# The fifth recurrent step of a four-layer graph network with tokens on the partitions: stationary data, moving weights, and no turn back of the state

## The chip, the core and the metric

The kernel runs on one NeuronCore of a Trainium2 chip. Five engines work side by side from queues of their own: TensorE (PE: matrix products and transposes into PSUM), VectorE (DVE), ScalarE (ACT), GpSimd (POOL) and SyncE (SP, which here only issues DMAs). The metric is the device time of one execution in microseconds. All data are float32.

## The reference, cut to what matters

There are 128 graphs of 64 nodes with 256 features each. Two attention layers come first, then a gated recurrent network (layer 2), then a gated graph convolution (layer 3). Every layer is a residual on a normalised input.

```python
h = relu(layernorm(x));  x = x + attention0(h, adj)
h = relu(layernorm(x));  x = x + attention1(h, adj)
# layer 2, five recurrent steps
h = relu(layernorm(x)); A = (adj != 0)
for l in range(5):
    m   = h @ weight[l]                    # 256 -> 256
    agg = einsum('bij,bid->bjd', A, m)     # sum over the neighbours
    gi  = agg @ w_ih.T + b_ih;  gh = h @ w_hh.T + b_hh     # 256 -> 3*256: r, z, n
    r, z = sigmoid(gi_r + gh_r), sigmoid(gi_z + gh_z)
    n   = tanh(gi_n + r * gh_n)
    h   = (1 - z) * n + z * h
x = x + h * nodemask
# layer 3
h = relu(layernorm(x)); norm = (sum(|adj|, -1) + 1e-6) ** -0.5
f_hom = adj @ ((h @ theta) * norm) * norm
gate  = sigmoid(h @ W_t + b_t)
x = x + elu(gate * f_hom + (1 - gate) * (h @ W_h))
```

## The kernel before, in words

Two graphs make a pair of 128 tokens, four pairs make a group of 512 tokens (`TOK`; `HALF` is 256), and there are 16 groups. `front(g)` does the two attention layers of group g, `entry` the normalisation ahead of the recurrent layer, `gru` its five steps (a generator that yields after each), and `back` layer 3 and the store.

The order of the instructions is written by a planner in the kernel (`class Plan`). Every operation is added with its engine, a cost in ns, what it reads and writes, and a due time (`key`). `strand` spreads the due times of a block over a share of a group's length. `Plan.run` then emits the operations in the order in which its own costs say that they can start, ties going to the earlier due time. The recurrent step l of group g has its due time at g + 0.4 l, so two groups are always inside the recurrent layer, and attention of a later group and layer 3 of an earlier one fill TensorE in between. The constants `FRONT_SPAN`, `BACK`, `STEP` and `LOCK` set these due times. The last group (`LOCK`) is drawn nearer to the one before.

Tiles come from `new(tag, shape, n)`: n buffers under a tag; a value waits until a buffer of its tag is free. There are four PSUM banks with tag `g` for the recurrent products (called `nb`, `gb`, `gc`, `nc` here) and four with tag `a` for everything else.

Inside the recurrent layer the state `h` lies with features on the partitions: `h[128 features, 2, 512 tokens]`. The products keep a 128x128 block of weights stationary and move 256 tokens of data (line 994). They use Strassen's scheme on 2x2 blocks: seven block products instead of eight, numbered 1 to 7, with the sums of data blocks in `Th` (of `h`) and `Ta` (of the aggregate), and sums of weight blocks prepared once in `w_hh` and `gv`. A block product is six matmuls in a step: r, z and n, each from `h` and from the aggregate. After a product an intermediate bank is copied to SBUF by ACT (`saved`, line 1058) and later added to another bank by DVE (`summed`, lines 1066 and 1069).

`update` (lines 1086 to 1107) then forms the gates and the new state for one half of the features: tanh on ACT with the bias b_rz, two DVE operations, tanh on ACT, a subtraction on POOL (line 1103), two DVE operations. After each step but the fifth, `turned` transposes `h` into `ht`, tokens on the partitions, because the aggregation `agg` (line 1034) wants it so. The last group's fifth step goes by halves of the tokens (`by_halves`, `update_half`) so that layer 3 can start on one half earlier.

Layer 3 wants tokens on the partitions. So `back_half` transposes the final `h` with TensorE into a PSUM tile `hx` (line 1375), and DVE adds it times the mask to x (line 1382). Layer 3 also needs each pair's adjacency as a block-diagonal 128x128 matrix, transposed: at the end of `front`, POOL copies the two 64x64 blocks into `blk` (line 1265), TensorE transposes them (line 1280) and ACT scales them into `adjT` (line 1285). `adjT` has four buffers, since it waits there until `back`, more than a group's length later.

The first groups also load and prepare the weights. SP issues nearly all DMAs from one queue, in the planner's order: among them the prepared gate weights `gv` once per step (line 977) and the attention weights `qw` (line 626).

Of the kernel before, what the change touches and what calls it, by code (L numbers as in the profile page):

```python
# [23 lines left out]
P = 128  # L24
# [37 lines left out]
FRONT_SPAN = 0.95  # L62
BACK = -0.1
BACK_LAST = 0.3
BACK_SPAN = 0.7
STEP = 0.0
STEP_LAST = -0.1
STEP_SPAN = 0.5
LOCK = 0.35
# [24 lines left out]
def act(n, ptr=0):  # L94
    return n * 0.833 + 60 + 105 * ptr
# [193 lines left out]
def network(ctx: ExitStack, tc: tile.TileContext, a: dict, out: bass.AP, flag):  # L289
# [99 lines left out]
    with plan.strand(-3.0, 0.1):  # L389
# [46 lines left out]
        first = [new("h", [P, 2, 2, D], 4, f"w_{n}") for n in ("qk0", "qk1", "v")]  # L436
# [21 lines left out]
        for c, tag in enumerate(("ht", "agg")):  # L458
            t = new(tag, [P, 3 * D], 2 if tag == "ht" else 1, f"w_ih{c}")
            dma(384, lambda c=c, t=t: nc.sync.dma_start(  # L460
                t.tile, a["L2_gnn_w_ih"][c * P : (c + 1) * P, :]), [], [t])
            w_ih.append(t)
# [42 lines left out]
    with plan.strand(-0.3, 0.1):  # L505
# [19 lines left out]
        b_t = load_row("L3_gnn_b_t")  # L525
        blk = filled("adjblk", [P, PAIRS, P], 0.0)
# [384 lines left out]
    def fuse_weights(l):  # L911
# [14 lines left out]
        for mc in range(2):  # L926
            for g0, n in ((0, 2), (2, 1)):
# [7 lines left out]
                def put(copy, mc=mc, g0=g0, n=n, ps=ps):  # L935
                    copy(gv[:, g0 : g0 + n, 2 * mc : 2 * mc + 2, :],
# [14 lines left out]
    def gru(h, ht, A, name, last=False):  # L951
# [20 lines left out]
        for l in range(LAYERS):  # L972
# [45 lines left out]
            hn(1, hi_b, True)  # L1018
            rz_h(1, rz_b, True)
            rz_h(2, rz_c, True)  # L1020
            hn(2, hi_c, True)
            Ta = new("Ta", [P, 4, HALF], 1, f"Ta_{nm}")

# [51 lines left out]
            ht2 = None if l + 1 == LAYERS else new("ht", [P, PAIRS, D], 2, f"ht_{nm}")  # L1075
# [34 lines left out]
            def turned(oc, ht2=ht2):  # L1110
                if ht2 is not None:
                    transposed(ht2, lambda: ht2[:, :, oc * P : (oc + 1) * P], h, lambda i: h[:, oc, i * P : (i + 1) * P],
                        f"hT_{nm}_{oc}", oc == 0, [(ht2, oc)],
                        reads=[(h, (oc, 0)), (h, (oc, 1))], width=P)

            def update_half(half, g_v, n_v, last=None):

                r, z, a_, b_ = (lambda v=v, k=k: v[:, :, k, :] for v in (g_v, n_v) for k in range(2))
                hh = lambda: h[:, :, half * HALF : (half + 1) * HALF]
                hp = [(h, (oc, half)) for oc in range(2)]  # L1120
                for k in range(2):
                    for oc in range(2):
                        src, at = (g_v, lambda k=k, oc=oc: g_v[:, oc, k, :]) if last is None or not oc else (
                            last, lambda k=k: last[:, k * HALF : (k + 1) * HALF])
                        col = 2 * k + oc
                        sca(act(HALF, 1.4), lambda k=k, col=col, oc=oc, at=at: nc.scalar.activation(
                            g_v[:, oc, k, :], at(), AF.Tanh, bias=b_rz[:, col : col + 1], scale=0.5),
                            [(src, oc) if src is g_v else src, b_rz], [(g_v, f"t{k}{oc}")])
                ts = [[(g_v, f"t{k}{oc}") for oc in range(2)] for k in range(2)]
                vec2(dve(TOK), lambda: nc.vector.scalar_tensor_tensor(  # L1130
                    a_(), r(), 1.0, a_(), op0=ALU.add, op1=ALU.mult), [*ts[0], n_v], [n_v])
                vec2(dve(TOK), lambda: nc.vector.scalar_tensor_tensor(
                    a_(), a_(), 0.5, b_(), op0=ALU.mult, op1=ALU.add), [n_v], [n_v])
                for oc in range(2):
                    sca(act(HALF, 1.4), lambda oc=oc: nc.scalar.activation(
                        n_v[:, oc, 0, :], n_v[:, oc, 0, :], AF.Tanh, bias=b_n[:, oc : oc + 1]), [n_v, b_n], [(n_v, oc)])
# [397 lines left out]
```

## Time and profile before

| | before |
|---|---|
| median of 6 runs | 2502.55 us (2501.34 to 2503.53) |
| the profiled execution | 2501.24 us |
| its span, first to last instruction | 2499.4 us |
| granted TensorE clock | 0.998 |
| PE / DVE / ACT / POOL busy | 2477.0 / 1881.6 / 1308.4 / 896.0 us |
| DMA, mean over the span | 75 GB/s |

A group line of the profile reads: source line, engine, operation, output<-inputs, shapes, count, then busy us and the mean ns of one, then the engine's idle time just ahead of them and who ended it. The count of a float32 matmul is two per matmul; a transpose counts once. The busy time of TensorE overlaps from one matmul to the next, so its pace is read from the starts in the timeline, not from the mean length of one. A timeline line reads: start, length, engine, source line, operation, output<-inputs, shapes, count.

### The profile page before, as it was taken

The numbers are of one execution on the slowest core, as the hardware profiler recorded it, in microseconds if no ns is written. First come the engines' busy times: TensorE is split into PE (matmuls) and PEld (weight loads), VectorE is DVE, ScalarE is ACT, GpSimd is POOL, SyncE is SP. The second block draws the span as 40 slices with busy tenths as digits, with TensorE's granted clock in tenths as the row PEclk, the third lists the DMA queues.
The fourth block names the chain that finished last, engine by engine and source line by source line (L and its number), as shares of the span: only waits on it lengthen the run. The fifth ranks groups of instructions, "written<-read, shape, count | busy, mean of one in ns | idle before, by whom it ended". The sixth has DMA issues, their size and how long they took to land.

```text
span 2499.4 us, 58765 instructions
## 1 busy us (share of the span) xinstructions
PE 2477.0 (99%) x24057; PEld 2130.3 (85%) x24057; DVE 1881.6 (75%) x4396; ACT 1308.4 (52%) x2654; POOL 896.0 (36%) x894
## 2 busy tenths in 40 slices
PE   9999999999999999999999999999999999999997
PEld 7788888888888888888888888888888888888885
DVE  6667777777777777787778777787777777777776
ACT  3455554555555455555555555555454555645544
POOL 5633433334233342433334233343333424332221
PEclk9999999999999999999999999999999999999999
DMA  6422212112222121212113122122211212212110
GB/s 210 159 71 86 72 53 99 65 53 84 72 80 72 60 76 66 98 54 80 59 63 102 50 95 76 52 82 72 80 68 60 76 66 80 68 50 71 51 69 19
DMA packets 78266, 188.60 MB, mean 75 GB/s; under 512 B 14802, under 2 KB 66852, under 8 KB 67108
## 3 DMA queue, kind: packets, MB, share of 16 engines
q1 hardware_dynamic: 77872, 184.71, 22.0%
q8 instruction: 192, 3.15, 0.5%
q14 instruction: 86, 0.70, 0.1%
q10 hardware_dynamic: 116, 0.04, 0.0%
HBM read 166.70 MB, written 18.02 MB: 74 GB/s over the span
## 4 chain that ended last, share of the span: by engine, by line
PE 98%; DVE 1%; ACT 1%; issue 0%; DMA 0%; POOL 0%; DVEq 0%; ACTq 0%
PE gb L994 22%; PE gc L994 17%; PE nb L994 11%; PE nc L994 8%; PE qkvb L711 6%; PE qkvc L711 5%; PE y L879 4%; PE agg L1034 3%; PE l3b L1339 3%; PE s L775 3%; PE l3c L1339 2%; PE hT L547 2%; PE lnT L547 2%; PE o L843 2%; PE o L851 1%; PE gv L930 1%
## 5 line engine op out<-in xcount | busy, mean ns | idle before, releaser
L1103 POOL TENSOR_TENSOR sn<-h,sn 128x512 f32<-128x512 f32 x158 | 202.9, 1287 | 544.5 <-ACT sn L1101 544.5
L533 POOL TENSOR_TENSOR rstd<-pw,few 128x2 f32<-128x2 f32 x128 | 96.3, 755 | 490.0 <-DVE pw L532 445.2
L994 PE MATMUL gb<-Th,w_hh 128*128 128x256 f32 x960 | 249.3, 382 | 0.0
L994 PE MATMUL gb<-Ta,gv 128*128 128x256 f32 x960 | 246.8, 380 | 0.0
L963 POOL TENSOR_TENSOR Th<-h 128x256 f32<-128x256 f32 x160 | 121.2, 777 | 299.6 <-PE nb L994 196.2
L799 POOL TENSOR_TENSOR e<-e,mask 128x512 f32<-128x512 f32 x128 | 177.4, 1406 | 111.5 <-ACT e L797 111.4
L994 PEld LDWEIGHTS gb<-Ta,gv 128*128 128x128 f32 x960 | 177.6, 190 | 22.1 <-issue 0.2
L994 PEld LDWEIGHTS gb<-Th,w_hh 128*128 128x128 f32 x960 | 175.7, 190 | 23.9 <-issue 2.4
L1101 ACT ACTIVATE sn<-sn,b_n 128x512 f32<-128x512 f32 x158 | 114.0, 722 | 143.8 <-DVE sn L1099 143.8
L1105 DVE SCALAR_TENSOR_TENSOR sn<-sg,sn 128x512 f32<-128x512 f32 x158 | 120.5, 769 | 74.4 <-POOL sn L1103 74.2
L994 PE MATMUL gc<-h,w_hh 128*128 128x256 f32 x640 | 167.7, 384 | 0.1
L994 PE MATMUL gc<-agg,gv 128*128 128x256 f32 x640 | 164.3, 379 | 0.0
L1086 ACT ACTIVATE sg<-sg,b_rz 128x512 f32<-128x512 f32 x158 | 106.5, 714 | 81.2 <-DVE sg L1066 81.2
L963 POOL TENSOR_TENSOR Th<-h,Th 128x256 f32<-128x256 f32 x160 | 144.9, 906 | 8.4 <-DVE h L1107 2.8
L552 ACT ACTIVATE hT<-lnT 128x512 f32<-128x512 f32 x96 | 57.1, 594 | 167.1 <-PE lnT L547 167.0
L994 PE MATMUL nb<-Ta,gv 128*128 128x256 f32 x480 | 144.0, 382 | 0.0
L994 PE MATMUL nb<-Th,w_hh 128*128 128x256 f32 x480 | 143.0, 380 | 0.0
L1097 DVE SCALAR_TENSOR_TENSOR sn<-sg,sn 128x512 f32<-128x512 f32 x158 | 117.7, 752 | 32.8 <-ACT sn L1208 28.3
L994 PEld LDWEIGHTS gc<-h,w_hh 128*128 128x128 f32 x640 | 116.2, 190 | 26.6 <-ACT sn L1208 4.0
L1099 DVE SCALAR_TENSOR_TENSOR sn<-sn 128x512 f32<-128x512 f32 x158 | 136.6, 871 | 2.4
L1047 DVE TENSOR_TENSOR Ta<-agg 128x256 f32<-128x256 f32 x160 | 100.2, 643 | 50.6 <-PE nb L994 27.7
L994 PEld LDWEIGHTS gc<-agg,gv 128*128 128x128 f32 x640 | 121.3, 190 | 16.7 <-issue 0.2
(228 smaller groups left out, 6560.4 us busy)
## 6 DMA issues: line engine op xcount, KB each, us to landing
gv<-gates SPq DMA_DIRECT2D x80, 1344.0 KB, 5.9
qw<-kept SPq DMA_DIRECT2D x203, 192.0 KB, 2.4
x<-in_x_dram SPq DMA_DIRECT2D x32, 256.0 KB, 3.0
out_dram<-x SPq DMA_DIRECT2D x32, 256.0 KB, 2.6
gates<-gv SPq DMA_DIRECT2D x5, 1344.0 KB, 5.6
adjq<-in_adj_dram SPq DMA_DIRECT2D x8, 256.0 KB, 4.7
gw<-in_L_gnn_weight_dram SPq DMA_DIRECT2D x5, 256.0 KB, 6.1
kept<-s SPq DMA_DIRECT2D x8, 128.0 KB, 1.8
```

The costliest lines, as they stand in the source:

```text
L711: nc.tensor.matmul(bk[:, j * P : (j + 1) * P], lhs, rhs, start=first and j == 0, stop=True, skip_group_check=True)
L799: pool(1225, lambda e=e: nc.gpsimd.tensor_tensor(e.tile, e.tile, bias_at(pp)[:, None, :].to_broadcast([P, 4, 2 * NODES]), op=ALU.mult), [e ...
L963: pool(690, lambda: nc.gpsimd.tensor_tensor(T[:, i, :], x(), y(), op=ALU.subtract), reads, [(T, i)])
L994: nc.tensor.matmul(bank_[:, col * HALF : (col + 1) * HALF], at(g, n), rhs(), start=first and j == 0, stop=True, skip_group_check=True)
L1047: vec2(dve(256), lambda: nc.vector.tensor_tensor(Ta[:, i, :], x(), y(), op=ALU.subtract), reads, [(Ta, i)])
L1086: sca(act(TOK, 1.5), lambda k=k, col=col: nc.scalar.activation(g_v[:, :, k, :], g_v[:, :, k, :], AF.Tanh, bias=b_rz[:, col : col + 1], sca ...
L1097: vec2(dve(TOK), lambda: nc.vector.scalar_tensor_tensor(a_(), r(), 1.0, a_(), op0=ALU.add, op1=ALU.mult), [*ts[0], n_v], [n_v])
L1099: vec2(dve(TOK), lambda: nc.vector.scalar_tensor_tensor(a_(), a_(), 0.5, b_(), op0=ALU.mult, op1=ALU.add), [n_v], [n_v])
L1101: sca(act(TOK, 1.5), lambda: nc.scalar.activation(a_(), a_(), AF.Tanh, bias=b_n[:, oc : oc + 1]), [n_v, b_n], [n_v])
L1103: pool(1230, lambda: nc.gpsimd.tensor_tensor(b_(), hh(), a_(), op=ALU.subtract), [*hp, n_v], [n_v])
L1105: vec2(dve(TOK), lambda: nc.vector.scalar_tensor_tensor(b_(), z(), 1.0, b_(), op0=ALU.add, op1=ALU.mult), [*ts[1], n_v], [n_v])
L1339: pe(mm(384), lambda: nc.tensor.matmul(bk[:, : 3 * P], b(), w3[:, :, n, :], start=first, stop=True, skip_group_check=True), [w3, *reads], ...
```

## The change

In the fifth step the operands change places. A block of 128 tokens of `h`, `agg`, `Th` or `Ta` is stationary, and the three gates' weights (3x128 columns) move, in `last_step`. A block product is then four matmuls of 384 columns (two blocks of 128 tokens, from `h` and from the aggregate) instead of six of 256. The result has tokens on the partitions, so the final state is formed in `ht`, in place, and `back_half` reads it without a transpose.

- In this layout a bias differs along the columns, so it cannot be ACT's per-partition bias. `load_b` spreads the biases over all partitions once, with six DMAs and one POOL addition into `b_row`. `saved` gets a POOL addition of `b_row` after each copy, six in a step. `summed` is four DVE additions of 256 columns in place of two of 512.
- One tanh of 1024 columns serves r and z of a half. The last group still goes by halves of tokens.
- `gv` of the fifth step holds the gates in the order n, r, z, so that the aggregate's part goes to columns 0 to 383 of a bank, and the state's (r, z, n) to 128 to 511.
- The transposed adjacency is made at the start of `back`. `blk` is filled there by two DMAs from HBM in place of POOL's two copies.
- Buffers: `h` 4 to 3, `ht` 2 to 3, `adjT` 4 to 2. Due times: `FRONT_SPAN` 0.95 to 1.0, `BACK` -0.1 to -0.05, `STEP` 0 to -0.05, `LOCK` 0.35 to 0.3.

```diff
-FRONT_SPAN = 0.95
-BACK = -0.1
+FRONT_SPAN = 1.0
+BACK = -0.05
...
-STEP = 0.0
+STEP = -0.05
...
-LOCK = 0.35
+LOCK = 0.3
...
+        b_row = new("b_row", [P, 2, 4, P], 1)
+        more = new("e", [P, 2, 2, P], 4 if lean else 3, "b_more")
+
+        def load_b():
+            ih, hh = a["L2_gnn_b_ih"], a["L2_gnn_b_hh"]
+            for dst, ap, at, gates in ((b_row[:, :, 0], ih, 2 * D, 0), (b_row[:, :, 3], hh, 2 * D, 0),
...
+                nc.sync.dma_start(dst, bass.AP(tensor=ap.tensor, offset=ap.offset + at, ap=[[0, P], [P, 2], [1, P]]))
+
+        dma(768, load_b, [], [b_row, more], 6)
+        pool(1225, lambda: nc.gpsimd.tensor_tensor(
+            b_row[:, :, 1:3, :], b_row[:, :, 1:3, :], more.tile, op=ALU.add), [b_row, more], [b_row])
...
+            by_token = l + 1 == LAYERS
+            if by_token:
+                tokens = last_step(nm, h, Th, Ta, agg, gv, ((rz_b, hi_b), (rz_c, hi_c)), operand, by_both, whole, last)
+                next(tokens)
+            else:
+                hn(1, hi_b, True)
...
+    def last_step(nm, h, Th, Ta, agg, gv, banks, operand, by_both, whole, halves):
+
+        def product(i, which, of_h, first=False):
+            n = WEIGHTS[i]
+            b, reads = operand(i, h, Th, by_both) if of_h else operand(i, agg, Ta, whole)
+            w = w_hh if of_h else gv
+            for t in range(2):
+                bk = banks[which][t]
+                pe(mm(384), lambda t=t, bk=bk: nc.tensor.matmul(
+                    bk[:, P:] if of_h else bk[:, : 3 * P], b()[:, t * P : (t + 1) * P], w[:, :, n, :],
+                    start=first, stop=True, skip_group_check=True), [w, reads], [bk])
...
+        def saved(which, n, oc):
...
+                sca(act(512), lambda c=c, bk=bk: nc.scalar.activation(
+                    c.tile, bk.tile.rearrange("p (g f) -> p g f", g=4), AF.Copy), [bk], [c])
+                pool(1225, lambda c=c: nc.gpsimd.tensor_tensor(c.tile, c.tile, b_row[:, oc], op=ALU.add),
+                     [c, b_row], [c])
...
+        def summed(oc, half, which, others):
...
+                for dst, key, part in ((sg, "g", lambda x: x[:, 1:3, :]), (sn, "n", lambda x: x[:, 0:4:3, :])):
+                    vec(dve(256), lambda dst=dst, part=part, bk=bk, p=p, o_at=o_at: nc.vector.tensor_tensor(
+                        dst[:, p], part(bk.tile.rearrange("p (g f) -> p g f", g=4)), part(o_at()), op=ALU.add),
+                        [bk, o], [(dst, p)])
...
+        def update(j):
...
+            sca(act(2 * TOK, 0.4), lambda: nc.scalar.activation(sg.tile, sg.tile, AF.Tanh, scale=0.5), parts, [sg])
...
+        if halves:
...
+            both(4, 0)
+            summed(1, 0, 0, None)
+            update(0)
+            both(5, 1, True)
+            summed(1, 1, 1, v)
+            both(3, 1)
+            summed(0, 1, 1, u)
+            update(1)
...
+        both(5, 1, True)
+        p5 = saved(1, "p5", 1)
+        both(6, 0)
+        u = saved(0, "u", 0)
+        both(3, 1)
+        summed(0, 1, 1, u)
+        update(0)
+        both(7, 0)
+        summed(1, 1, 0, p5)
+        both(4, 0)
+        summed(1, 0, 0, None)
+        update(1)
...
-        for gp in range(2):
-            s = slice(gp * NODES, (gp + 1) * NODES)
-            pool(350, lambda s=s: nc.gpsimd.tensor_copy(blk[s, :, s], adjq[s, sel, :]), [adjq], [(blk, gp)])
-
...
+    def back(g, xt, norm):
+
+        def fill():
+            for gp in range(2):
+                s = slice(gp * NODES, (gp + 1) * NODES)
+                nc.sync.dma_start(blk[s, :, s], adj_t[s, g * PAIRS : (g + 1) * PAIRS, :])
+
+        dma(128, fill, [], [blk], 2)
+        adjT = new("adjT", [P, PAIRS, P], 2, f"adjT_{g}")
...
-    def back_half(g, xt, h, adjT, norm, half):
-        ps = bank(f"hx_{g}_{half}")
-
-        def turn():
-            for i in range(2):
-                for c in range(2):
-                    t0 = (2 * half + i) * P
-                    nc.tensor.transpose(ps[:, i * D + c * P : i * D + (c + 1) * P],
-                                        h[:, c, t0 : t0 + P], ident.tile)
-
-        pe(437, turn, [(h, (0, half)), (h, (1, half)), ident], [ps], mode=TURN)
...
-                xt[:, p, :], ps[:, i * D : (i + 1) * D], cols[:, 18 + t : 19 + t], xt[:, p, :],
-                op0=ALU.mult, op1=ALU.add), [ps, cols, (xt, p)], [(xt, p)])
+    def back_half(g, xt, adjT, norm, half):
+        h_by_token = final[g]
+        for p in range(2 * half, 2 * half + 2):
...
+                xt[:, p, :], h_by_token[:, p, :], cols[:, 18 + t : 19 + t], xt[:, p, :],
+                op0=ALU.mult, op1=ALU.add),
```

## The prediction

> **What bounds the kernel now.** I read the page's busy shares and its chain first, then the windows by group, then the starts in TensorE's timeline, then the waits and the groups that the change touches.
>
> ```profile
> PE 2477.0 (99%) x24057; PEld 2130.3 (85%) x24057; DVE 1881.6 (75%) x4396; ACT 1308.4 (52%) x2654; POOL 896.0 (36%) x894
> PE 98%; DVE 1%; ACT 1%; issue 0%; DMA 0%; POOL 0%; DVEq 0%; ACTq 0%
> ```
>
> TensorE is busy nearly always and is 98% of the chain that ended last. The windows (length, then busy us by engine) show that this holds in each stage but the end:
>
> ```profile
> 912.00:1064.00 152.00, 152.00 (x1504) 131.65 (x1503) 117.44 (x278) 81.51 (x168) 54.57 (x54) 1.00 0.22 74
> 1064.00:1216.00 152.00, 152.00 (x1505) 131.83 (x1504) 117.46 (x278) 81.63 (x168) 54.65 (x54) 1.00 0.22 72
> 2432.00:2499.40 67.40, 49.57 (x264) 35.21 (x262) 47.30 (x117) 29.89 (x64) 9.99 (x13) 0.94 0.05 18
> ```
>
> A group takes 152 us and repeats itself; DVE has 34 us of slack in it, ACT 70, POOL 97. The clock is 1.00. What TensorE issues is what a group costs. Its pace stands in the starts:
>
> ```profile
> 329.55 0.81 PE L1339 MATMUL l3c<-w,hTT 128*128 128x384 f32 x2
> 330.20 0.81 PE L1339 MATMUL l3b<-w,hTT 128*128 128x384 f32 x2
> 330.84 0.59 PE L994 MATMUL nb<-Th,w_hh 128*128 128x256 f32 x2
> 331.27 0.81 PE L1339 MATMUL l3c<-w,hT 128*128 128x384 f32 x2
> ...
> 999.71 0.81 PE L994 MATMUL gb<-h,w_hh 128*128 128x256 f32 x3
> 1000.45 1.16 PE L1034 MATMUL agg<-A,ht 64*64 64x64 f32 x64
> ```
>
> Two records of 384 columns take 0.645 us from start to start, so 322.5 ns each; two of 256 take 0.43, so 216 each. The 384 rows are layer 3's: data stationary, weights moving with a stride, which is the form that the fifth step gets. Their weight load (190 ns) hides. The three records ahead of `agg` take 0.74 and not 0.65: entering small tiles costs 0.09 us.
>
> ```profile
> L1375 PE MATMUL hx<-ident,h 128*128 128x128 f32 x128 | 19.2, 274 | 1.4 <-DVE h L1141 1.4
> L1103 POOL TENSOR_TENSOR sn<-h,sn 128x512 f32<-128x512 f32 x158 | 202.9, 1287 | 544.5 <-ACT sn L1101 544.5
> L1047 DVE TENSOR_TENSOR Ta<-agg 128x256 f32<-128x256 f32 x160 | 100.2, 643 | 50.6 <-PE nb L994 27.7 <-ACT sg L1093 20.6 <-ACT agg L1040 2.2
> L1265 POOL COPY adjblk<-adjq 64x256 f32<-64x256 f32 x32 | 19.3, 603 | 4.8 <-PE adjT L1280 3.4 <-DMA adjq<-in_adj_dram 0.4
> PE f L1310 <- ACT hT L552: 2.2, 2, 1.1
> PE hx L1375 <- DVE h L1141: 1.4, 1, 1.4
> ```
>
> The last two are waits (total, times, longest). The usual steps between starts, summed over the order before, make 2439.5 us; first to last start takes 2485.3. So 45.8 us are waits: 9.7 in the first 152 us, 2.7 in the second, 1.4 to 2.0 in each later one, 7.5 after 2432. The end is short of work on TensorE, so chains over DVE and ACT count there. The span of 2499.4 stands in an execution of 2501.24, 1.3 under the median 2502.55; the sum below is made on the span and taken off the median.
>
> **The change, part by part.** First TensorE, counted in the order of both programs.
>
> Fifth step: out go 16 x 42 = 672 matmuls of 256, two records each: 1344 x 216 ns = 290.3 us. In come 16 x 28 = 448 of 384: 896 x 322.5 = 289.0. Net -1.3: the columns are the same, only the fixed few ns become fewer.
>
> The turn back: 128 transposes go. Four of them pace 0.43 us in the timeline, 109 ns each: -13.9. TensorE is the bound where they stand, so all of it counts.
>
> Adjacency: the same 64 transposes, moved from `front` to `back`: 0. Their POOL copies go (32 x 0.60 = 19 us on an engine with slack).
>
> Small tiles: the planner's order of the changed kernel goes 152 times from full to small tiles, before 138. 0.09 on entering, and 0.1 to 0.2 on leaving (148 to 199 ns where one small record follows another in 7 to 38): 14 x 0.2 = +2.8, at most 14 x 0.3 = 4.2.
>
> Sum on TensorE: -1.3 - 13.9 + 2.8 = -12.4 us, or -0.7 us a group.
>
> Other engines, a group. POOL gets 6 additions like L1103 (1.29, mask product 1.41) and loses two copies: 7.7 - 1.2 = +6.5 on 54.7 of 152. DVE gets 16 additions of 256 from PSUM (0.42 each, as layer 3's copy shows) for 6 of 512 (0.69): +2.6 on 117.5. ACT loses a copy of 0.69 and trades eight tanh for four longer ones: -2. None gets near 152: no price by itself, the cover is TensorE's 150 us. What is left is latency.
>
> (1) `saved` is longer by two POOL additions in a row, 2.6 us. After product 1 the order has 11 us of TensorE work before product 5 overwrites the banks: cover enough (copies 1.2 + additions 2.6 + sums 1.4 = 5.2). After product 6 `u` has 4.3 us until the second bank of product 3 is to be summed, against 0.8 + 2.6 plus POOL's queue, where a mask product (1.41) may stand ahead: slack from +0.9 to -0.5. Behind it are the banks that the next group's step starts with, at once. Bounds: 0, and one POOL addition plus what a DVE operation with two SBUF inputs loses (643 - 414 alone = 0.23) less 0.5, so 1.0 a group, 14 us in all. I take 0.15 x 14 = +2, near the low end, since most waits of that length are covered today.
>
> (2) Beside POOL a DVE operation with two SBUF inputs is slow already: L1047 takes 643 ns on average, 414 where no POOL operation overlaps. Twelve percent more POOL work makes the existing excess 12% larger: well under 1 us of DVE's slack.
>
> The Trainium skill (SBUF — State Buffer, section "SBUF: two separate sides") says that VectorE and GpSimd hold their shared port as an exclusive lock for the whole instruction, which speaks against six more POOL additions; if each blocked DVE for its full 1.29 us, an estimate from that rule, DVE would come to 128 of 152 us, still no bound, and the sum would stay -12.4 plus whatever of it lies on a chain.
>
> (3) SP: the fill is two more DMAs a group (64 KB each, 256-byte runs) right behind the turn of the group before, some 140 us of TensorE work ahead of its use. The adjacency load of 256 KB in the same runs lands in 4.7 us. `blk` has one buffer, so SP waits there for that turn, with the next group's `gv` queued behind; 14 us of TensorE steps remain until that group's first product, against 0.9 of issue and `gv`'s 5.9 to land. Price 0; if the turn came 7 us late, `gv` would be late by what is over. The six bias loads stand where SP's timeline is empty (46 to 53 us) and the addition on POOL waits for them: 0, at most their landing of about 4 us. Fewer `h` buffers: the first loads leave theirs by 63 us and `h` is first written near 93.
>
> The Trainium skill (DMA: Bandwidth & Descriptors, section "Specifications") puts line rate at 512 bytes and more; by it the fill is slow, which its 140 us of cover make worth nothing.
>
> (4) The start: `adjT` leaves a stretch with 0.6 of waits, other work is reshuffled: 0, bounds -3 and +3.
>
> (5) The end. From product 4 of the last group to layer 3's turn `lnT` of its first half the trace takes 14.2 us (2457.0 to 2471.2), 12.5 of them TensorE work, 1.7 waits. In the new order only 9.9 us of TensorE work stand there; more was put ahead. The chain loses `hx` and its wait for TensorE (about 1), tanh becomes one of about 0.93 for four of 0.41 to 0.46 (-0.8), and DVE, packed there, gets 12 starts of 256 at 0.34 for 4 of 512 at 0.62 (+1.6). I get 13.3 by walking it, so a wait of 3.4: +1.7 against before. Bounds: 9.9 (no wait, -1.7) and 15.8 (nothing saved, +4.2). The two waits of `f` (2.2) stay.
>
> Sum: -12.4 + 2 + 0 + 1.7 = -8.7, or rounded with the many bounds at zero -9: **2493.5 us**.
>
> **The rivals.** All of TensorE's gain arrives and the chain at the end is no longer than today's: -12.4, perhaps -1.7 on top: 2488.5 to 2490. For it: a group repeats with 1.75 us of waits, most of about 0.1. Against: the thin end.
>
> Slower: `u` waits for POOL in each group. Place: the last sums of product 3 in the fifth step. Price: a whole addition late behind a mask product, 1.41 + 0.23, and the next group's first products with it; 16 x 1.64 = 26 on -12.4 gives 2516. It decides from 0.78 us a group (12.4 / 16). For it: POOL is in order, and DVE waits up to 2.5 us for its L1103 today. Against: POOL is 40% busy and the step has filler.
>
> No change within 0.2% (5 us either way, about what can be told): the same waits at 0.5 to 0.8 a group, or a start and an end both at their upper bounds (+3, +4.2, +1.4 small tiles): 2499 to 2503.
>
> That the turn back was hidden anyway would give 2507 (13.9 less gained); against it, TensorE waits only 1.8% of the time (45.8 of 2485.3), so there is hardly a gap that a transpose could have filled.
>
> **How the numbers follow.** Forecast 0.55 (own range 2490.5 to 2497), full gain 0.22 (2487 to 2490.5), no change 0.13 (2497.5 to 2507), slower 0.10 (2507 to 2520). Two in ten left out are the slow case and half of no change, so 2487 to 2501. Faster than 2497.5: 0.55 + 0.22 + 0.01 = 0.78; same 0.12; slower 0.10.
>
> **What would show it.** Groups that repeat every 151.3 to 151.5 us; no `hx` line; the fifth step's records at 322 ns start to start; TensorE's waits still near 1.8 us a group; a wait of `lnT` or its neighbour of 2 to 5 us at the end. I am wrong if sums of the fifth step stand idle for POOL, with TensorE's `nb` or `gb` of the next step waiting for them, or if the first 300 us grow.

## The result, and the profile after

The changed kernel takes 2508.53 us in the median of 17 runs (2507.28 to 2511.52), the kernel before 2501.76 in 37 (2501.02 to 2503.72). The ratio is 1.0026, with a 95% interval of 1.0020 to 1.0033: it is slower by nearly 7 us (0.26%), where 9 fewer were forecast. The profiled execution took 2507.86 us with a span of 2505.9, at a clock of 0.997.

The first and the fourth part of the page of the changed kernel, the busy shares and the chain that ended last:

```profile
PE 2474.8 (99%) x23481; PEld 2033.3 (81%) x23481; DVE 1920.9 (77%) x4556; ACT 1284.0 (51%) x2570; POOL 990.9 (40%) x959
PE 94%; DVE 2%; issue 1%; ACT 0%; POOL 0%; DVEq 0%; ACTq 0%
```

TensorE has 576 records fewer, and yet its share of the chain fell from 98% to 94%: it waits more. GpSimd (POOL) has 95 us more to do. The windows of the same groups as before (length, then busy time of PE, PEld, DVE, ACT and POOL with their counts, clock, DMA share, GB/s):

```profile
912.00:1064.00 152.00, 151.12 (x1460) 124.81 (x1460) 119.36 (x285) 80.15 (x162) 59.83 (x57) 1.00 0.21 73
1064.00:1216.00 152.00, 151.30 (x1466) 125.32 (x1465) 119.65 (x287) 80.24 (x162) 59.74 (x58) 1.00 0.22 74
2432.00:2505.90 73.90, 56.88 (x256) 35.31 (x254) 55.64 (x135) 31.35 (x64) 20.32 (x20) 0.89 0.05 16
```

Before, TensorE was busy for all of the 152 us of such a window; now 0.7 to 0.9 us are gaps. The waits of TensorE in the changed kernel (engine, what waited, for what: us in total, times, longest) name them:

```profile
PE nb L1012 <- DVE sn L1221: 7.7, 11, 0.7
PE hom L1471 <- DVE F L1391: 2.9, 1, 2.9
PE f L1384 <- ACT hT L567: 1.8, 2, 1.1
```

The first line is new. L1012 is the product of a recurrent step (L994 before), L1221 is `summed` in the fifth step: `nb` of the next group's third step waits for its bank until a sum of the fifth step has read it out, 11 times, once in each of groups 2 to 12. Counted as in the prediction, the usual steps between TensorE's starts sum to 2427.0 us instead of 2439.5, which is 12.5 less; 12.4 was forecast. From the first to the last start 2493.0 us pass instead of 2485.3. So the waits are 66.0 us and not 45.8: +20.2. Of these some 12.9 lie at that place (11 times 1.17, with the products right behind it), 3 to 4 in the last 80 us, up to 1.6 in the first 300 (this goes by what one calls a usual step), and about 3 in late small tiles, of which more below (these overlap by about 1). What follows the last start became 1.2 shorter. -12.5 + 20.2 - 1.2 is the 6.5 by which the span grew.

The place itself, in the timeline of the changed kernel (start, length, engine, line; the groups look alike, this is the change of step near 902 us):

```profile
899.09 2.49 POOL L1209 TENSOR_TENSOR u<-u,b_row 128x512 f32<-128x512 f32 x2
...
901.53 0.71 POOL L548 TENSOR_TENSOR rstd<-pw,few 128x2 f32<-128x2 f32 x1
901.78 0.42 DVE L1221 TENSOR_TENSOR sg<-gc,u 128x256 f32<-128x256 f32 x1 [0.75 <-PE gc L1194]
...
902.12 1.55 DVE L710 TENSOR_TENSOR hTQ<-hT 128x128 f32<-128x128 f32 x2
...
902.21 1.31 POOL L803 TENSOR_TENSOR x<-x,r_L_gnn_bo 128x512 f32<-128x512 f32 x1
...
903.60 0.28 DVE L710 TENSOR_TENSOR hTQ<-hT,hTQ 128x128 f32<-128x128 f32 x1
903.80 0.41 DVE L1221 TENSOR_TENSOR sn<-gc,u 128x256 f32<-128x256 f32 x1
...
904.36 0.67 PE L1012 MATMUL nb<-h,w_hh 128*128 128x256 f32 x2 [0.70 <-DVE sn L1221]
```

Read it from below. `nb` waits for the second sum, `sn<-gc,u`. That sum does not wait for anything: between the two sums VectorE (DVE) has instructions of an attention layer of a later group, the subtractions `hTQ` (L710), whose time is 0.28 each elsewhere. Here two of them take 1.55 (one alone 1.36), and they end at 903.67, just behind GpSimd's addition L803 (903.52). The trace has 11 such subtractions, one at each of the 11 places; all end 0.15 us behind an L803. L803 adds the bias `bo` to x ahead of attention's output (L788 before, called x + bo below). It comes here because GpSimd, which takes its instructions one after the other, is behind: from 899.09 on it has done the two new bias additions of `u` (L1209), an `rstd` (L548) and then L803. And `u` was not late: its additions were over at 901.58, and the first sum waited until 901.78 for TensorE's `gc`.

How far a GpSimd instruction holds one of VectorE shows in two more rows of the trace, the instructions of single tiles with min/median/max in ns. `pw_deg` adds a constant to a tile of 128x4. Before:

```profile
L532 DVE TENSOR_SCALAR pw_deg<-deg x16: 156/158/960, 10.4 to 2020.2; 128x4 f32<-128x4 f32 x16
```

After, in the first row, and below it `hTQ`:

```profile
L547 DVE TENSOR_SCALAR pw_deg<-deg x16: 161/1236/1245, 8.8 to 2055.5; 128x4 f32<-128x4 f32 x16
...
L710 DVE TENSOR_TENSOR hTQ<-hT x116: 248/281/1365, 84.5 to 2221.5; 128x128 f32<-128x128 f32 x116
```

The 11 long `pw_deg` all start 0.3 to 0.6 us behind an L803 and end 0.02 to 0.03 us behind its end. The one that starts 0.02 us ahead of a GpSimd instruction (300.37, the subtraction L1248) takes 169 ns.

### The profile page after: what moved, and what is told of

The parts are those of the page before. It is cut to its first block, busy times and chain, and to the rows that moved or that the text cites. A ratio compares the mean times of both kernels' runs of the same rounds, so it can differ in the third digit from the quotient of the medians.

```text
span 2505.9 us, 57822 instructions
## 1 busy us (share of the span) xinstructions
PE 2474.8 (99%) x23481; PEld 2033.3 (81%) x23481; DVE 1920.9 (77%) x4556; ACT 1284.0 (51%) x2570; POOL 990.9 (40%) x959
## 4 chain that ended last, share of the span: by engine, by line
PE 94%; DVE 2%; issue 1%; ACT 0%; POOL 0%; DVEq 0%
PE gb L1012 18%; PE gc L1012 13%; PE nb L1012 9%; PE nc L1012 7%; PE qkvb L726 6%; PE qkvc L726 4%; PE y L894 4%; PE gb L1194 3%; PE agg L1057 3%; PE nb L1194 3%; PE l3b L1413 3%; PE s L790 3%; PE gc L1194 2%; PE hT L562 2%; PE l3c L1413 2%; PE nc L1194 2%
## 5 line engine op out<-in xcount | busy, mean ns | idle before, releaser
L1126 POOL TENSOR_TENSOR sn<-h,sn 128x512 f32<-128x512 f32 x128 | 163.4, 1277 | 714.7 <-ACT sn L1124 714.2
L548 POOL TENSOR_TENSOR rstd<-pw,few 128x2 f32<-128x2 f32 x128 | 107.6, 841 | 324.1 <-DVE pw L547 314.0
L1012 PE MATMUL gb<-Th,w_hh 128*128 128x256 f32 x768 | 199.9, 383 | 0.0
L1012 PE MATMUL gb<-Ta,gv 128*128 128x256 f32 x768 | 197.6, 380 | 0.0
L1012 PEld LDWEIGHTS gb<-Ta,gv 128*128 128x128 f32 x768 | 143.0, 190 | 23.8
L1012 PEld LDWEIGHTS gb<-Th,w_hh 128*128 128x128 f32 x768 | 140.4, 190 | 21.9 <-issue 4.7
L1128 DVE SCALAR_TENSOR_TENSOR sn<-sg,sn 128x512 f32<-128x512 f32 x128 | 110.1, 860 | 48.9 <-POOL sn L1126 48.7
L894 PE MATMUL y<-w_L_gnn_Wo,oT 128*128 128x256 f32 x512 | 138.4, 380 | 0.1
L1012 PE MATMUL gc<-h,w_hh 128*128 128x256 f32 x512 | 131.9, 380 | 0.2 <-DVE h L1130 0.2
L1012 PE MATMUL gc<-agg,gv 128*128 128x256 f32 x512 | 131.5, 379 | 0.0
L1012 PE MATMUL nb<-Ta,gv 128*128 128x256 f32 x384 | 115.5, 382 | 0.0
L1012 PE MATMUL nb<-Th,w_hh 128*128 128x256 f32 x384 | 114.5, 380 | 0.0
L1070 DVE TENSOR_TENSOR Ta<-agg 128x256 f32<-128x256 f32 x160 | 93.8, 603 | 25.0 <-ACT sg L1116 19.5
L592 DVE TENSOR_SCALAR xn<-x,mv,rstd 128x256 f32<-128x256 f32 x192 | 103.5, 567 | 11.9 <-POOL rstd L548 6.1
L894 PEld LDWEIGHTS y<-w_L_gnn_Wo,oT 128*128 128x128 f32 x512 | 93.0, 190 | 23.3 <-issue 1.2
L726 PEld LDWEIGHTS qkvb<-hTQ,qw 128*128 128x128 f32 x696 | 100.2, 191 | 12.9 <-DVE v L747 0.2
L726 PE MATMUL qkvb<-hTQ,qw 128*128 128x128 f32 x696 | 106.5, 275 | 0.0
```

What stands on the lines that cost most here:

```text
L548: pool(660 if n == 2 else 970, lambda: nc.gpsimd.tensor_tensor(dst.tile, s.tile, few[:, 1 : 1 + n], op=ALU.pow), [s, (few, 1)], [dst], port=2)
L592: vec2(325, lambda p=p, i=i: nc.vector.tensor_scalar(xn[:, i, :], xt[:, p, :], mv_at()[:, i, 0:1], rstd[:, i : i + 1], op0=ALU.subtract, o ...
L726: nc.tensor.matmul(bk[:, j * P : (j + 1) * P], lhs, rhs, start=first and j == 0, stop=True, skip_group_check=True)
L894: pe(mm(256), lambda i=i, c=c: nc.tensor.matmul(py[:, i * D : (i + 1) * D], oT[:, i, c, :], w_o[:, c, :], start=c == 0, stop=c == 1), [(oT ...
L1012: nc.tensor.matmul(bank_[:, col * HALF : (col + 1) * HALF], at(g, n), rhs(), start=first and j == 0, stop=True, skip_group_check=True)
L1070: vec2(dve(256), lambda: nc.vector.tensor_tensor(Ta[:, i, :], x(), y(), op=ALU.subtract), reads, [(Ta, i)])
```

## The experiments

In the texts below, theory A is this: GpSimd comes late to the change of step; its x + bo holds an `hTQ` between two sums that free a bank; `nb` waits. Rivals: the sums wait for the additions themselves (B); TensorE became slower in itself (C); VectorE is too full in any order (D). In the table, "waits" is the time from TensorE's first to last start less its usual steps, in us.

| kernel | median us | ratio to before, 95% | waits |
|---|---|---|---|
| before | 2501.76 | | 45.8 |
| changed | 2508.53 | 1.0026 (1.0020 to 1.0033) | 66.0 |
| x + bo short | 2495.78 | 0.9977 (0.9967 to 0.9987) | 54.2 |
| before, x + bo short | 2503.07 | 1.0003 (0.9994 to 1.0012) | 47.2 |
| bias additions short | 2496.60 | 0.9979 (0.9970 to 0.9988) | 55.8 |
| second sum moved up | 2507.09 | 1.0021 (1.0012 to 1.0030) | 63.4 |
| four sums first | 2499.79 | 0.9992 (0.9983 to 1.0001) | 57.4 |
| pairs of sums planned as one | 2510.45 | 1.0045 (1.0031 to 1.0058) | 69.2 |
| truer costs for the planner | 2521.46 | 1.0077 (1.0063 to 1.0091) | 80.6 |
| old constants | 2520.71 | 1.0076 (1.0063 to 1.0090) | 76.5 |
| x + bo later | 2505.15 | 1.0014 (1.0005 to 1.0023) | 62.7 |
| x + bo later, four sums first | 2513.79 | 1.0046 (1.0032 to 1.0060) | 72.8 |
| no fill of the adjacency | 2508.32 | 1.0026 (1.0016 to 1.0037) | 65.1 |
| four sums first, subtraction on VectorE | 2496.63 | 0.9979 (0.9970 to 0.9988) | 56.2 |
| subtraction on VectorE alone | 2507.27 | 1.0020 (1.0011 to 1.0030) | 64.7 |
| x + bo later, subtraction on VectorE | 2497.50 | 0.9980 (0.9971 to 0.9989) | 53.8 |
| four sums first, subtraction on VectorE, long stretches split | 2496.68 | 0.9979 (0.9970 to 0.9988) | 54.0 |

Where a line of the table says "short", the order of all instructions is that of its parent: the planner was given the same costs. Each ratio is to runs of the kernel before made beside that kernel, with medians between 2501.36 and 2502.16 us; a difference of under 1 us between two lines tells nothing.

**x + bo short.**

```diff
-            xt[:, pp : pp + 2, :], xt[:, pp : pp + 2, :], bo[:, None, :].to_broadcast([P, 2, D]),
+            xt[:, pp : pp + 2, :8], xt[:, pp : pp + 2, :8], bo[:, None, :8].to_broadcast([P, 2, 8]),
```

> The changed kernel with its order of instructions untouched, in which GpSimd's addition x + bo (L803) covers 8 of each row's 256 columns, so that it takes a fraction of its 1.35 us; the other columns go without that bias, and nothing else is changed. Theory A (the port): in the changed kernel this addition runs late, between the two sums of the fifth step that free bank gc, and holds VectorE's second hTQ subtraction for 1.36 us instead of 0.28; TensorE's nb of the next group waits for it, 11 times 1.17 = 12.9 us. Then this run is 11 to 14 us under the changed kernel, about 2496, and the waits of nb on sn are below 0.3 us a group. Rival B (the six additions of b_row are what is late, and the sums wait for them): x + bo stands behind them in GpSimd's queue, and the time stays within 2 us of 2508.5. Rival C (TensorE itself got slower, in its weight loads or its rate): no change either.

2495.78 us, 12.7 less than the changed kernel. The same place in this run's timeline:

```profile
898.11 0.42 DVE L1221 TENSOR_TENSOR sg<-gc,u 128x256 f32<-128x256 f32 x1 [0.75 <-PE gc L1194]
...
898.46 0.50 DVE L710 TENSOR_TENSOR hTQ<-hT 128x128 f32<-128x128 f32 x2
...
898.54 0.27 POOL L803 TENSOR_TENSOR x<-x,r_L_gnn_bo 128x16 f32<-128x16 f32 x1
...
898.88 0.28 DVE L710 TENSOR_TENSOR hTQ<-hT,hTQ 128x128 f32<-128x128 f32 x1
899.08 0.41 DVE L1221 TENSOR_TENSOR sn<-gc,u 128x256 f32<-128x256 f32 x1
```

The pair of `hTQ` takes 0.50 instead of 1.55, the second sum starts 0.97 after the first and not 2.02, and `nb` no longer stands among the waits. Since the order is the same, the starts of TensorE's records in the two traces can be set side by side: this run gains 1.02 to 1.03 us at each of the 11 places, 11.3 us in all (of the 1.17 there, 0.15 stays). It gains 1.0 once more near 147 us, in an ordinary step, where x + bo holds two other VectorE instructions (`Ta`, L1070: 1.92 us together instead of 0.87). C falls, and so does B, since the additions are as long as before.

**The same in the kernel before.** The same edit, at line 788 there.

> The kernel before with the same addition (there L788) on 8 of 256 columns, the other columns going without that bias; its order is untouched. It tells what a short x + bo is worth where it does not stand between two sums. Theory A: within 2 us of 2501.8. If GpSimd's use of the port costs TensorE something everywhere, it gains as much here as in the changed kernel, and theory A falls.

2503.07 us, no shorter than before. A short x + bo is worth nothing where it lies elsewhere; in the changed kernel it is the place that costs.

**Bias additions short.**

```diff
-nc.gpsimd.tensor_tensor(c.tile, c.tile, b_row[:, oc], op=ALU.add)
+nc.gpsimd.tensor_tensor(c[:, :, :4], c[:, :, :4], b_row[:, oc, :, :4], op=ALU.add)
```

> The changed kernel, order untouched, with the additions of b_row to the copied banks (L1209, 96 of them) on 4 of each block's 128 columns; the other columns go without that bias. Theory A says that these additions only make GpSimd late, so that x + bo falls between the sums: with them short it ends before the first sum, nb no longer waits, and the run is 11 to 14 us under the changed kernel, about 2496. Rival B (sums wait for the additions) says the same of this run, and no change of the run with x + bo short: the two together tell them apart. Rival C: no change, 2508.

2496.60 us, 11.9 less. By TensorE's starts it gains 1.02 to 1.04 us at each of the same 11 places (11.3 us), while the hold near 147 us stays: it is none of the additions' doing. So the six additions a group are what makes GpSimd late, and x + bo is how that reaches TensorE: either one taken away brings the same 11.3 us at these places.

**Second sum moved up.** One VectorE instruction a group changes its place.

```diff
...
+                if others and others[0].name.startswith("u"):
+                    sides = (lambda one=one: (one(sg, lambda x: x[:, 1:3, :]), one(sn, lambda x: x[:, 0:4:3, :])),
+                             lambda: None)
...
```

> The changed kernel with one VectorE instruction a group put elsewhere: the second sum of gc with u (into sn) is issued directly behind the first (into sg), ahead of the two hTQ subtractions that stood between them; all other instructions of all engines in the same order, all computation kept. Theory A: bank gc comes free about 1 us sooner, nb waits 0.3 us or less, the run is 9 to 13 us under the changed kernel, 2496 to 2500, and what the subtractions lose is hidden. If the subtractions, now later, hold up the products of layer 1 of the next group, the gain is less by up to 1 us a group. Rival B and C: within 2 us of 2508.5.

A miss: 2507.09 us, only 1.4 less, which the intervals do not tell from nothing. From the waits of TensorE in this run:

```profile
PE gb L1012 <- DVE sn L1221: 8.4, 11, 0.8
```

And VectorE in its timeline at the place:

```profile
902.33 1.37 DVE L710 TENSOR_TENSOR hTQ<-hT 128x128 f32<-128x128 f32 x2
903.62 0.28 DVE L710 TENSOR_TENSOR hTQ<-hT,hTQ 128x128 f32<-128x128 f32 x1
903.82 0.41 DVE L1221 TENSOR_TENSOR sg<-nc,u 128x256 f32<-128x256 f32 x1
904.15 0.41 DVE L1221 TENSOR_TENSOR sn<-nc,u 128x256 f32<-128x256 f32 x1
```

`nb` has its bank now, but `gb`, 0.5 us later, needs the bank `nc`, which the third and fourth sums free, and these stand behind the held `hTQ`.

**Four sums first.** The `hTQ` subtractions that fall between the sums with `u` are issued behind the fourth.

```diff
-                vec2(dve(128), lambda n=n, x=x, y=y: nc.vector.tensor_tensor(T[:, n, :], x(), y(), op=ALU.subtract),
+                later = lambda n=n, x=x, y=y: nc.vector.tensor_tensor(T[:, n, :], x(), y(), op=ALU.subtract)
+                vec2(dve(128), lambda later=later: behind.append(later) if held_back[0] else later(),
                     [hT, *reads], [(T, n)])
...
```

> The changed kernel with the two hTQ subtractions a group (groups 1 to 11) issued behind all four sums with u instead of between the first and second; nothing else moves on any engine, all computation kept. Moving only one sum won 1.4 us: the wait went from nb to gb, whose bank nc is freed by the sums behind the subtractions (8.4 us in 11 waits instead of 7.7). Theory A (what counts is the subtraction held by GpSimd's x + bo ahead of the last of four sums): now both banks are free before x + bo matters, the waits on sn go from 7.7 us to under 1, and the run is 10 to 13 us under the changed kernel, 2495.5 to 2498.5. Rival D (VectorE is simply too full here, whatever the order): the wait turns up a third time, at layer 1's products behind hTQ, and the run stays above 2505.

2499.79 us, 8.7 less, 1.3 outside what was expected. The wait on the sums with `u` is gone from both banks, so D does not hold. But 11 short waits of about 0.25 (2.7 us) turned up 7 to 8 us later, at the fifth step's `gb<-w_hh,Th`.

**Three orders that the planner makes itself.** Pairs of sums planned as one job; costs nearer to the rows (1300 for 1225, 800 for 660); the four constants as they were before.

```diff
...
+                vec(2 * dve(256), pair, [bk, o], [(sg, p), (sn, p)])
```

> The changed kernel with each pair of sums (sg and sn of one bank) given to the planner as one job of VectorE of twice the cost: the planner makes another order, in which no hTQ stands between the sums of u, and no stretch of small TensorE tiles is longer than 144 (176 in 12 groups in the changed kernel). The usual steps of TensorE's matmuls add up to 2425.5 us in this order (2427.0 in the changed kernel, 2439.5 before). Theory A: 2494 to 2498, nb does not wait on sn. Theory of the long stretch (s of L790 is slow at the end of 176 small tiles, 24 records over 70 ns late, 3.8 us): fewer than 10 such records here. Rival D: other waits take the place, above 2503.

```diff
...
-                pool(1225, lambda c=c: nc.gpsimd.tensor_tensor(c.tile, c.tile, b_row[:, oc], op=ALU.add),
+                pool(1300, lambda c=c: nc.gpsimd.tensor_tensor(c.tile, c.tile, b_row[:, oc], op=ALU.add),
...
-        pool(660 if n == 2 else 970, lambda: nc.gpsimd.tensor_tensor(dst.tile, s.tile, few[:, 1 : 1 + n], op=ALU.pow),
+        pool(800 if n == 2 else 970, lambda: nc.gpsimd.tensor_tensor(dst.tile, s.tile, few[:, 1 : 1 + n], op=ALU.pow),
```

> The changed kernel with the planner told GpSimd's times nearer to the rows: 1300 instead of 1225 for x + bo and the additions of b_row (they take 1.34), 800 instead of 660 for rstd (0.84). Again another order, with one short pw between the sums of u; steps of TensorE add up to 2425.8 us; no stretch of small tiles over 144. Theory A (the planner believed GpSimd done before it was): 2494 to 2498. Rival D: above 2503.

```diff
-FRONT_SPAN = 1.0
-BACK = -0.05
-STEP = -0.05
-LOCK = 0.3
+FRONT_SPAN = 0.95
+BACK = -0.1
+STEP = 0.0
+LOCK = 0.35
```

> The changed kernel with the four constants of the planner as they were before (FRONT_SPAN 0.95, BACK -0.1, STEP 0, LOCK 0.35). The order has no hTQ between the first two sums of u, in odd groups one hTQ before the last two; TensorE's usual steps add up to 2431.0 us, 4.0 above the changed kernel and 8.5 under before. Theory A: no wait of 0.87 at nb in the even groups, perhaps a short one in the odd groups, 2496 to 2504. If the constants only shift work that is hidden, 2508.

Three misses: 2510.45, 2521.46 and 2520.71. In none does `nb` wait 0.7 for the sums with `u`, as theory A has it, but each order has waits of its own. The largest wait for another engine with the sums planned in pairs:

```profile
PE hT L562 <- DVE h L1130: 3.5, 1, 3.5
```

With the truer costs:

```profile
PE lnT L562 <- DVE xn L592: 4.7, 5, 2.3
```

With the old constants:

```profile
PE gb L1012 <- ACT agg L1063: 7.7, 6, 1.3
```

In the first two the last 80 us hold 19 and 21 us of waits (11.2 in the changed kernel, 7.5 before). Of the late `s` tiles 3 are left with the pairs, as expected, but there and with the truer costs `o` tiles come late instead (3.8 and 5.1 us without a releaser). What caused these waits was read and not tried. What is shown: the same change under the old constants costs 12 us more, and the truer costs did not make the better order here.

**x + bo later.** GpSimd issues x + bo behind the next `rstd`, if a bias addition of `u` stands just ahead.

```diff
...
+            if kind == "bo" and since_u[0] <= 2:
+                waits.append(fn)
+                return
             fn()
+            while waits:
+                waits.pop(0)()
...
```

> The changed kernel with only GpSimd's x + bo of groups 1 to 12 moved: it is issued behind the next rstd instead of right behind the bias additions of u, so that it runs some 4 us later, with no sum to come; VectorE's and TensorE's instructions are in the same order, all computation kept. Theory A: hTQ is not held, the second sum follows after 0.3 us, nb does not wait: 10 to 13 us under the changed kernel, 2495.5 to 2498.5, like the run with a short x + bo (2495.8), and 4 us under the run that moved the subtractions (2499.8) if it leaves the later x + bo beside nothing that matters. Rival E (any place of x + bo in this stretch holds some other two-operand instruction of VectorE on the way to the next products): 2500 to 2508.

Then the same together with the edit of the four sums.

> Both moves at once: x + bo behind the next rstd, and the two hTQ subtractions behind the four sums with u. Theory A: the two cure the same wait, so that together they win no more than the better one: 2495 to 2499. If they were two separate costs, the gains would add up, to about 2488.

2505.15 us, 3.4 less, and with both moves 2513.79, 5.3 more than the changed kernel: two misses, and the second told most. The waits on sums were 5.4 us in the first and 14.4 in the second, all at `gb<-w_hh,Th` some 8 us after the place above. From the first one's timeline (its lines are shifted by 12: L1265 is the changed kernel's L1253, L1260 is L1248, L1233 is `summed`):

```profile
907.18 1.27 POOL L1260 TENSOR_TENSOR sn<-ht,sn 128x512 f32<-128x512 f32 x1
...
908.48 0.69 DVE L1265 SCALAR_TENSOR_TENSOR sn<-sg,sn 128x512 f32<-128x512 f32 x1 [1.23 <-POOL sn L1260]
...
909.09 0.42 DVE L1233 TENSOR_TENSOR sg<-gb,p 128x256 f32<-128x256 f32 x1
...
909.42 0.42 DVE L1233 TENSOR_TENSOR sn<-gb,p 128x256 f32<-128x256 f32 x1
...
909.98 0.88 PE L1206 MATMUL gb<-w_hh,Th 128*128 128x384 f32 x2 [0.48 <-DVE sn L1233]
```

This is a second chain. GpSimd subtracts the new candidate from the state (L1260), VectorE's next instruction waits for that, and behind it in VectorE's queue stand the sums with `p5`, which free `gb` and `nb` for the step's product 4. In the changed kernel VectorE waits there too (38.6 us in 25 times at that instruction), though `gb` does not yet wait for it. A later x + bo delays GpSimd there, and that reaches TensorE.

**No fill of the adjacency.**

```diff
-                nc.sync.dma_start(blk[s, :, s], adj_t[s, g * PAIRS : (g + 1) * PAIRS, :])
+                if g == 0:
+                    nc.sync.dma_start(blk[s, :, s], adj_t[s, g * PAIRS : (g + 1) * PAIRS, :])
```

> The changed kernel with the two transfers that fill the block adjacency from memory left out in all groups but the first, so that layer 3 uses the first group's adjacency everywhere; all else in the same order. The prediction took these transfers as free. If so: within 2 us of 2508.5, and the late small tiles (s of L790, 24 records over 70 ns, 3.8 us) stay. If the transfers slow the fetching of TensorE's small instructions, those records go and the run is 2 to 4 us shorter.

2508.32 us against 2508.53, and the same 24 late tiles. The transfers cost nothing that can be measured.

**Subtraction on VectorE.** The planner keeps its place and its cost; only the engine that executes it is another.

```diff
-                pool(1230, less(nc.gpsimd), [*before, sn], [sn])
+                pool(1230, less(nc.vector), [*before, sn], [sn])
```

> As in the run with the four sums first, and besides that the state's subtraction in the fifth step of all groups but the last (L1248, sn <- ht, sn) issued on VectorE instead of GpSimd, at the same place of the order. Theory A2 (two chains hang on a late GpSimd: x + bo holds the hTQ subtraction ahead of the sums with u; and L1248 ends late, VectorE's L1253 waits for it, and behind L1253 in VectorE's queue stand the sums with p5 that free gb and nb): four sums first left 11 waits of about 0.25 at gb, 3.0 us; they go, and the run is 2495 to 2498, below the kernel before by 0.15 to 0.3%. If the second chain is none, the added 0.68 us a time on VectorE does nothing or harm: 2500 to 2505.

> The changed kernel with that subtraction on VectorE, and nothing else moved. Theory A2: the first chain is earlier in the group and stays, nb waits as before (7.7 us in 11), and the run is 2506 to 2509. If GpSimd's total load alone were the cause, 30 instructions of 1.28 fewer, 38 us, would bring it under 2503.

> The run with x + bo behind the next rstd (2505.2, its wait gone from nb to the later gb, 5.4 us in 11 waits on sn and 7.5 with what follows), with the subtraction on VectorE. Theory A2: x + bo is now late where nothing on VectorE's queue waits for GpSimd: the waits at gb go, 2496.5 to 2499.5. Rival: x + bo beside VectorE's own operations there costs as much, 2502 to 2505.

2496.63, 2507.27 and 2497.50 us, each within what was expected. Alone it wins 1.3 us, no more than the intervals can tell, for the first chain is untouched. With either cure of the first chain it wins the rest: 3.2 on top of four sums first, 7.7 on top of the later x + bo. No wait on a sum of the fifth step is left. The subtraction (L1262 here) in the first of these runs, now on VectorE, with the sums with `p5` (L1228) behind it:

```profile
905.17 0.68 DVE L1262 TENSOR_TENSOR sn<-ht,sn 128x512 f32<-128x512 f32 x1
905.88 0.69 DVE L1267 SCALAR_TENSOR_TENSOR sn<-sg,sn 128x512 f32<-128x512 f32 x1
906.64 0.42 DVE L1228 TENSOR_TENSOR sg<-gb,p 128x256 f32<-128x256 f32 x1
```

The first and the third are faster than the changed kernel and the kernel before, the first at 0.9979 (0.9970 to 0.9988) of the latter.

**Long stretches split.** In 12 groups of the changed kernel 64 `agg`, 80 `o` and 32 `s` tiles follow each other with no wide matmul between; the longest such stretch before is 144. The `s` tiles are issued one product later; otherwise it is the kernel with four sums first and the subtraction on VectorE.

```diff
...
+            if mode == T64 and cost == 840 and small[-2:] == [T64, T32]:
+                put_off.append(fn)
+                return
...
```

> The kernel of the run with four sums first and the subtraction on VectorE, with the 32 score tiles that stand behind 64 agg and 80 o tiles (176 small tiles in a row, in 12 groups) issued one product later, so that wide matmuls part them; TensorE's usual steps grow by 1.1 us. In the changed kernel the tiles of these 12 stretches come 6.1 us late in sum, up to 1.6 a stretch, with no wait to be seen. If the length of the stretch causes it, at most 2 us of that stay and the run is 2 to 3.5 us shorter than its twin without the move; if not, it is 1 us longer.

2496.68 us, the same as its twin (2496.63), which neither view expected. In the trace the late `s` tiles (over 70 ns) go from 24 to 3 and the waits fall by 2.2 us, but the usual steps grow by 1.1, and the rest of about 1 us is within what the medians can tell.

The starts also show that length alone does not make a stretch late. Of the 12 in the changed kernel eight take the same 3.21 us; the four at 507, 965, 1270 and 1728 us take 0.56 to 1.0 longer, 2.8 us in all. The DMA records of the trace fit this. The page counts them as:

```profile
q8 instruction: 188, 3.08, 0.5%
```

These are 188 transfers of 16 KB of instructions, one for about 250 recorded TensorE instructions (matmuls and weight loads together; a stretch of 176 tiles has 352). In the four late stretches one of them starts within the first 1.05 us, in the other eight at 1.47 us or later. In the eleven traces with the changed kernel's order on TensorE and in the split run, 40 small tiles come over 0.25 us later than is usual at their place, after the first 300 us; all 40 start 2.2 to 2.9 us behind the start of such a transfer. So TensorE seems to run out of fetched instructions there. This is read from the traces; no run tried it.

## Why the prediction was wrong

The step that failed is (1), the price of the six additions: "+2", taken near the low end of 0 to 14 us. It measured 12 (11.9 with the additions short, 11.3 of it at the 11 places; 12.7 with x + bo short, which takes away also the 1.0 near 147 us), near the upper end. That 12 lies within the bounds at all is luck: they were made for a late `u`, and `u` was not late.

- **Its slack was right and asked the wrong question.** It gave `u` a slack of +0.9 to -0.5 us, and `u` was in time by 0.2. But GpSimd takes its instructions in order, so six additions delay also what stands behind them. That is x + bo, and in some orders L1248. The prediction prices neither; of L1248 it says only, in the slower rival, that VectorE waits for it (as L1103) before the change. What waits for `u` was named ("the banks that the next group's step starts with"), what stands behind the additions in GpSimd's queue was not.
- **The hold was sized by an average.** "643 - 414 alone = 0.23" is the mean loss over 160 instructions, of which 105 take less than 0.46 us, while 15 take over 1.0, up to 2.4. One that is held lasts to the end of the other: 1.36 instead of 0.28, a loss of 1.08. A single hold counts where it stands ahead of a bank.
- **Step (2) looked at VectorE's total.** "Well under 1 us of DVE's slack" is a statement on 152 us; the hold sits between two sums. It also spoke only of operations with two SBUF inputs. `pw_deg`, with one tile and a constant, went from a median of 158 ns to 1236.
- The Trainium skill says in SBUF — State Buffer, section "SBUF: two separate sides", that whoever has the shared port keeps it for the whole instruction and the other one stops fully. The trace agrees: each of the 11 held `hTQ` ends 0.15 us behind x + bo, after 1.36 us. The prediction cited this and let it end in "plus whatever of it lies on a chain", without looking for that chain.
- The page VectorE: DVE Perf Modes, section "Mode 2×_2P — use both read ports for one tensor", says that an operation on one SBUF tile and a constant can use both read ports. That fits the row of `pw_deg`; no run here tells whether it is the reason.

What held:

- **TensorE's sum of -12.4.** Counted in the trace: -12.5 (over 16 groups that is -0.78 a group; the prediction's "-0.7" is rounded down). The fifth step's records follow each other at 322.5 ns (902.18 to 902.82 is two of them), and no `hx` is left. With the wait out of the way it shows in the time: 2495.8 and 2496.6, within the range given and 2 to 3 us above the forecast. The transposes `adjT` of one group and the next lie 152.0 us apart before and mostly 152.3 in the changed kernel; with x + bo short it is mostly 151.3, the repeat that the prediction named.
- **The fill and the bias loads at 0**: without the fills 2508.3 against 2508.5. **The start at 0**: at most 1.6 us more of waits in the first 300, inside -3 to +3.
- **The end.** From product 4 to `lnT` of the first half: 13.0 us against 13.3 walked, with 2.9 of wait against 3.4. The changed kernel's timeline there:

```profile
2475.81 0.67 PE L1471 MATMUL hom<-F,adjT 128*128 128x256 f32 x2 [2.88 <-DVE F L1391]
2476.32 0.99 PE L562 MATMUL lnT<-ident,xn 128*128 128x128 f32 x4
```

  The last 80 us hold 3 to 4 us more of waits than before and the tail is 1.2 shorter: some +2 to +2.5 where +1.7 was put.
- **Of the rivals** the slower one named the right engine and nearly the right place, but a wait that did not occur (`u` behind a mask product). Its turning point, 0.78 us a group over 16 groups, was nearly reached by another wait: 11.9 / 16 = 0.74.
- **What would show it wrong** named `nb` waiting for the sums of the fifth step. It came so, except that the sums did not stand idle for GpSimd: they stood behind an instruction that did.

Two things were not foreseen at all: about 3 us of late small tiles, and that the waits depend on the planner's order more than on the edit. Eight kernels with the same instructions on the same engines, in other orders, run from 2499.8 to 2521.5 us.

## What to carry to other kernels

When work is added to an engine that is far from full, list what stands behind it in that engine's queue, not only who waits for the added result; the bill came from an old instruction pushed to a bad place. Price a hold between GpSimd and VectorE as a whole instruction at one spot, and ask for each such spot whether a read that frees a PSUM bank stands behind it. When a moved wait only changes its name, shrink the suspected instructions in place, order untouched: that told what the chain was worth (12 us), and each move could be judged against it.

## What the runs showed that was not expected

- A VectorE instruction of 128x4 elements takes 1236 ns instead of 158 beside a GpSimd addition of 1.5 us that had started 0.3 us earlier; one 32 times as large (128x128) was held for 1365 ns beside an addition of 1.3 us. The wait goes by what is left of the GpSimd instruction, not by the size of the held one.
- Small tiles can come late with no releaser in the trace. It was always the same four of the 12 stretches of 176, in every kernel with that order, but by other amounts each time (842, 1252, 1240 and 1241 ns at one tile; nearly nothing in one of the four stretches in two runs). Parting the stretches removed most of it. The adjacency transfers are not the cause; the transfers of instructions fit it, as read above, but no run tried them.
- Moving one bank's sums ahead won at most 1.4 of 12 us, since two banks, freed half a microsecond apart, gate the same product sequence.
